# Reordering one step of a convolution stage: TensorE's taps ahead of the rows, the rows' copy behind ScalarE's taps, a silu between two taps

## The chip, the cores and the metric

The kernel runs on one core of one Trainium2 chip. The metric is device microseconds of that core for the whole program. The core's engines work side by side, each through its own list of instructions: TensorE (PE in the profile, with its weight loads as PEld), VectorE (DVE), ScalarE (ACT), GpSimd (POOL) and SyncE (SP), which here only issues DMAs. GpSimd issues DMAs of its own.

## What is computed

Two layers over 8 images of 128 x 128 positions and 128 channels, all in float32. The first is a linear attention with a normalisation. The second is a state space layer; its beginning, which the change is about, is a projection to 256 channels, a depthwise 3 x 3 convolution, a silu, and a small projection to 10 rows:

```
xz = x @ Win
xb, z = jnp.split(xz, 2, axis=-1)
xb = jnp.transpose(xb, (0, 3, 1, 2))
xb = jax.lax.conv_general_dilated(xb, conv_w, (1, 1), ((1, 1), (1, 1)), ..., feature_group_count=Cd)
xb = jax.nn.silu(xb + conv_b[None, :, None, None])
xf = xb.reshape(Bb, Cd, L)
xt = jnp.transpose(xb, (0, 1, 3, 2)).reshape(Bb, Cd, L)
xs = jnp.stack([xf, xf[..., ::-1], xt, xt[..., ::-1]], axis=1)
...
x_dbl = jnp.einsum('bcl,cd->bdl', xs_flat, Wxproj)
dt = x_dbl[:, :r]
Bs = x_dbl[:, r:r + N]
Cs = x_dbl[:, r + N:]
```

Four scans over the positions, a gate, a normalisation and an output projection follow.

## The kernel before

The program has three stages: layer0 (to about 2400 us of the profiled span), layer1_front (to about 4540 us) and layer1_scan (the rest). The change is in layer1_front alone.

The front goes through 8 images in 16 pieces of 1024 positions (8 columns of 128), which makes 128 steps n. The 256 channels are two halves, c = 0 and c = 1, of 128 partitions each. A helper, in_order, ties the instructions of every engine to the order in which the program issues them, so the order in step(n) is the order on each engine's queue, SP's and GpSimd's included. An engine that waits holds all that stands behind it.

What is done for a piece n, with the function names and lines:

- load(n) (L481, SP): its columns of x1 into one of two buffers xi.
- project(n, c) (L488, TensorE): into a PSUM tile pxb of which there is one buffer. place(n, c) (L497, ScalarE) copies it into the bordered tile xb, and a second small copy (L502) writes the edge columns shared by the pieces n and n-1, so VectorE's last two taps of piece n-1 need place(n, c).
- The nine taps of the convolution are divided. taps_pe (L515, TensorE) computes two from xi with premultiplied weights into a PSUM tile acc, of which there are two buffers; so the taps of piece n+1 wait for the silu of the same half of piece n. taps_act (L523, ScalarE) scales three shifted copies of xb into tiles tap, and GpSimd adds them up (L525, two additions). taps_dve (VectorE) adds that sum to acc (L531) and does four multiply-adds (L533).
- silu(n, c) (L538, ScalarE) reads acc and writes ures, in which a whole image is kept.
- rows(n) (L547, TensorE) multiplies ures with the 10-row projection into a PSUM tile pr. keep_rows(n) (L551, ScalarE) copies pr into the one tile xd, and SP issues two stores of it (L554). spread(n, hf) (L559, TensorE) turns a row of xd into tiles pb, and by_b(n) (L568, VectorE) multiplies ures with them in place and stores the result (L569, SP). pr, pb and ptx, a tile of turned parts, take turns in two PSUM buffers.
- sum_d(n) (L582, ScalarE) writes du, which is stored or, in 6 of 8 images, added by GpSimd's DMA (L590).
- turn(k) (L605) copies a turned part of the image out of ures, two per step, and store_turned (L612, SP) stores it; two buffers are in turn. In the same 6 of 8 images ScalarE does half of one of the two ("shared").
- In some steps of an image parts of stored rows are loaded (L623), split by GpSimd (L44, L46) or turned by TensorE (L636) and copied by ScalarE (L638), and stored (L646).

step(n) works on several pieces at once: VectorE on n, by_b on n-1, ScalarE's taps on n+1, the load on n+2. In the kernel before, rows(n) stands at the end of step n and keep_rows(n) near the start of step n+1, ahead of ScalarE's taps.

Of the kernel before, what the change touches and what calls it, by code (L numbers as in the profile page):

```python
# [383 lines left out]
def layer1_front(ctx: ExitStack, tc, x1, win, conv_w, conv_b, wxp, d_par, ubs, xds, xps, gs):  # L384
# [20 lines left out]
    ON_ACT = ((-1, -1), (-1, 0), (-1, 1))  # L405
# [8 lines left out]
    def weight(n, c, dw, dh):  # L414
        i = tap(dh, dw) if own(place_of(n)[0]) == TURN else tap(dw, dh)
        return cw[:, c, i : i + 1]
# [54 lines left out]
    def place_of(n):  # L471
        return SEQ[n // NCH % B], n % NCH
# [3 lines left out]
    def load(n):  # L476
        b, g = place_of(n)
        x = xins[n % 2]
        cols = CW + 1 if g < NCH - 1 else CW
        src = x1[b].rearrange("c (w h) -> c w h", h=H)[:, g * CW : g * CW + cols, :]  # L480
        nc.sync.dma_start(x[:, 0:cols, inner], src)  # L481
        if g == NCH - 1:
            nc.gpsimd.memset(x[:, CW, :], 0.0)

    def project(n, c):
        pxs[n, c] = px = pj.tile([P, CW, H], F32, name="pxb", tag="pj")
        for hf in range(2):
            nc.tensor.matmul(  # L488
                px[:, hf * 4 : hf * 4 + 4, :], wi[:, c, :], xins[n % 2][:, hf * 4 : hf * 4 + 4, inner],
                start=True, stop=True,  # L490
            )

    def place(n, c):

        g = n % NCH
        xb = xbs[n % 2]
        nc.scalar.copy(xb[:, c, 1 : CW + 1, inner], pxs.pop((n, c)))  # L497
        if g == 0:
            nc.gpsimd.memset(xb[:, c, 0, :], 0.0)  # L499
        else:  # L500
            dst, src = edges[n % 2]
            nc.scalar.copy(dst[:, c], src[:, c])  # L502
        if g == NCH - 1:
            nc.gpsimd.memset(xb[:, c, CW + 1, :], 0.0)

    def at(n, c, dw, dh):
        return xbs[n % 2][:, c, 1 + dw : 1 + dw + CW, 1 + dh : 1 + dh + H]

    def taps_pe(n, c):
        accs[n, c] = acc = pa.tile([P, CW, H], F32, name="acc", tag="acc")  # L510
        for hf in range(2):
            s = slice(hf * 4, hf * 4 + 4)
            for j, (dw, dh) in enumerate(ON_PE):
                x = xins[n % 2][:, hf * 4 + dw : hf * 4 + dw + 4, 1 + dh : 1 + dh + H]
                nc.tensor.matmul(acc[:, s, :], wt[:, j, c, :], x, start=(j == 0), stop=(j == len(ON_PE) - 1))  # L515

    def taps_act(n, c):
        for j, d in enumerate(ON_ACT):
            if j:
                t = wp.tile([P, CW, H], F32, name="tap", tag="tb", bufs=4)  # L520
            else:
                t = wp.tile([P, CW, H], F32, name="tap", tag="ta", bufs=2)
            nc.scalar.activation(t, at(n, c, *d), AF.Copy, scale=weight(n, c, *d))  # L523
            if j:
                nc.gpsimd.tensor_tensor(sums[n, c], sums[n, c], t, ALU.add)  # L525
            else:
                sums[n, c] = t

    def taps_dve(n, c):
        acc = accs[n, c]  # L530
        nc.vector.tensor_tensor(acc, sums.pop((n, c)), acc, ALU.add)  # L531
        for d in ON_DVE:
            nc.vector.scalar_tensor_tensor(acc, at(n, c, *d), weight(n, c, *d), acc, ALU.mult, ALU.add)  # L533

    def silu(n, c):
        g = n % NCH
        u = ures[:, c, g * CH : g * CH + CH]
        nc.scalar.activation(u, accs.pop((n, c)).rearrange("p w h -> p (w h)"), AF.Silu, bias=cb[:, c : c + 1])  # L538

    def rows(n):  # L540

        g = n % NCH
        prs[n] = p = pm.tile([2 * 32, 512], F32, name="pr", tag="m")
        for c in range(NC2):
            for hf in range(2):
                u = ures[:, c, g * CH + hf * 512 : g * CH + hf * 512 + 512]
                nc.tensor.matmul(p[32 * hf : 32 * hf + 32, :], wx[:, c, :], u, start=(c == 0), stop=(c == NC2 - 1))  # L547

    def keep_rows(n):
        b, g = place_of(n)  # L550
        nc.scalar.copy(xd[0:64, :], prs.pop(n))  # L551
        for hf in range(2):
            s = slice(g * CH + hf * 512, g * CH + hf * 512 + 512)
            nc.sync.dma_start(xds[b][:, s], xd[32 * hf : 32 * hf + R + 2, :])  # L554

    def spread(n, hf):
        pbs[n, hf] = p = pm.tile([P, 1, 512], F32, name="pb", tag="m")
        sel = ident[:, 32 * hf + R : 32 * hf + R + 1].to_broadcast([P, P])
        nc.tensor.matmul(p[:, 0, :], sel, xd, start=True, stop=True)  # L559

    def by_b(n):

        b, g = place_of(n)
        dst = ubs[b, own(b)].rearrange("c p l -> p c l")
        for hf in range(2):
            s = slice(g * CH + hf * 512, g * CH + hf * 512 + 512)
            u = ures[:, :, s]
            nc.vector.tensor_tensor(u, u, pbs.pop((n, hf)).to_broadcast([P, NC2, 512]), ALU.mult)  # L568
            nc.sync.dma_start(dst[:, :, s], u)  # L569
# [14 lines left out]
    def store_sum(n):  # L584
        if place_of(n)[0] in SEQ_FIRST:
            nc.sync.dma_start(sums_at(n), dus.pop(n))

    def add_sum(n):
        if place_of(n)[0] not in SEQ_FIRST:
            nc.gpsimd.dma_start(sums_at(n), dus.pop(n), accum_op=ALU.add)  # L590
# [6 lines left out]
    def turn(k, copies, tag, bufs):  # L597
        m, r = divmod(k, COPIES)
        hf = m % 2
        c, i = divmod(r, COPIES // NC2)  # L600
        turned[k] = t = wp.tile([P, 2 * 8, HALF], F32, name="turned", tag=tag, bufs=bufs)
        rows = 16 // len(copies)
        for j, copy in enumerate(copies):
            r0 = 16 * i + rows * j
            copy(t[:, rows * j : rows * j + rows], uturn[:, c, r0 : r0 + rows, hf * HALF : hf * HALF + HALF])  # L605

    def store_turned(k):
        m, r = divmod(k, COPIES)
        b, hf = SEQ[m // 2], m % 2
        c, i = divmod(r, COPIES // NC2)  # L610
        dst = ubs[b, 1 - own(b)][c].rearrange("p (g e q) -> p g e q", e=2, q=8 * HALF)[:, 2 * i : 2 * i + 2, hf, :]
        nc.sync.dma_start(dst, turned.pop(k).rearrange("p (g h) w -> p g (h w)", g=2))  # L612

    def shared(n):
        return 0 <= n < N and place_of(n)[0] not in SEQ_FIRST
# [25 lines left out]
    def store_parts():  # L641
        while parts:
            q, r0, rows, order, p = parts.pop(0)
            dst = xps[SEQ[q], order if own(SEQ[q]) == NAT else 1 - order].rearrange("j r (a e) -> a j r e", e=P)
            for j in range(3):
                nc.sync.dma_start(dst[:, j, r0 : r0 + rows, :], p[:, j])  # L646
# [16 lines left out]
    def step(n):  # L663

        live, then, later, before = 0 <= n < N, 0 <= n + 1 < N, 0 <= n + 2 < N, 1 <= n <= N
        b, g = place_of(n)
        ka, kb = 2 * (n - 8) - 1, 2 * (n - 8)
        if live:
            taps_dve(n, 0)
        if ka >= 0:  # L670
            turn(ka, [nc.gpsimd.tensor_copy], "tc", 2)
        if before:
            add_sum(n - 1)
        if before:
            keep_rows(n - 1)
        if live:
            taps_pe(n, 1)
        if later:
            load(n + 2)
        if then:  # L680
            project(n + 1, 1)
            taps_act(n + 1, 0)
            place(n + 1, 1)
        store_parts()
        if before:
            store_sum(n - 1)
        for k in sorted(turned):
            if k != ka:
                store_turned(k)
        if before:  # L690
            for hf in range(2):
                spread(n - 1, hf)
        if live:
            silu(n, 0)
        if then:
            taps_pe(n + 1, 0)
        if later:
            project(n + 2, 0)
        if live:
            taps_dve(n, 1)  # L700
        if then:
            taps_act(n + 1, 1)
        if ka >= 0:
            store_turned(ka)
        if before:
            by_b(n - 1)
        if live:
            silu(n, 1)
        if later:
            place(n + 2, 0)  # L710
        if live:
            rows(n)
            sum_d(n)
        if kb >= 0:
            turn(kb, [nc.gpsimd.tensor_copy, nc.scalar.copy] if shared(n) else [nc.gpsimd.tensor_copy], "tc", 2)
        split_step(n)
# [19 lines left out]
    with in_order(tc):  # L736
        for n in range(-2, N + 1):
            step(n)
        tail()
# [523 lines left out]
```

## Time and profile before

| | |
|---|---|
| median of 3 runs | 9363.71 us (9353.22 to 9363.73) |
| profiled execution | 9364.78 us, span 9363.0 us |
| busy in the span | DVE 85%, POOL 78%, ACT 76%, PE 68% |
| stretch 3400 to 3800 us (in the front) | DVE 354.73, PE 350.49, ACT 345.20, POOL 337.89 us busy of 400; DMA 0.84 |
| front, first and last L531 of VectorE | 2407.45 and 4522.59 us |

Shares over the whole span mix three stages with different limits; for this change only the stretch of the front counts. There all four engines are busy for 84% to 89% of the time, so that none is clearly the limit, and the order of the work and the waits between the engines set the length of a step. A step is about 16.5 us: (4522.59 - 2407.45) / 128. A row of the waits names who waited, for whom, and for how long in total. This one is SyncE's, whose issue of a store stands for a while in every step before ScalarE has copied the rows:

```profile
SPq L554 <- ACT xd L551: 761.2, 128, 18.4
```

The columns are total us, times, longest us.

### The profile page before, as it was taken

Reading aid. Unit: us, or ns where it says so; the run is one execution under the profiler, and the core shown is the slowest. Engines: PE = TensorE matmul, PEld = TensorE weight load, DVE = VectorE, ACT = ScalarE, POOL = GpSimd, SP = SyncE. Lnnn points to the kernel's source line nnn. Section 1 sums busy time; section 2 is a strip of 40 time slices with the busy share of each in tenths; the row PEclk is TensorE's granted clock in tenths of the full one; section 3 lists DMA queues with packets and bytes.
Section 4 is the critical chain, followed back from the end, with each engine's and each line's share of the span. In section 5 each row is a group of like instructions: output and inputs, shape, how many; then the busy total and the mean of one; then the engine's idle time right before and its main releaser. Section 6 shows DMA issues by size and latency. Waiting matters only on the chain. (4 is left out here: it accounts for less than half of the span.)

```text
span 9363.0 us, 91413 instructions
## 1 busy us (share of the span) xinstructions
PE 6381.8 (68%) x24512; PEld 3145.7 (34%) x24512; DVE 7997.6 (85%) x7953; ACT 7096.1 (76%) x8066; POOL 7319.3 (78%) x4684
## 2 busy tenths in 40 slices
PE   8899998998888988888434636436364363643636
PEld 5555555554333333333101403114031140321403
DVE  6667666674799988888799999999999999999996
ACT  5555555658788888888688787887888878788885
POOL 3446444465688888888589899998999989999997
PEclk9999999999999999999655756657575575665857
DMA  1322333223477788888757759578595785967858
GB/s 75 144 91 90 134 118 144 105 80 143 159 240 239 249 233 230 234 233 225 215 155 208 234 169 260 166 204 239 167 267 166 206 234 165 252 175 200 248 165 216
DMA packets 934771, 1750.67 MB, mean 187 GB/s; under 512 B 150229, under 2 KB 376149, under 8 KB 926065
## 3 DMA queue, kind: packets, MB, share of 16 engines
q1 hardware_dynamic: 873328, 1509.92, 48.8%
q0 software_dynamic: 60928, 234.90, 13.5%
q8 instruction: 200, 3.28, 0.1%
q14 instruction: 315, 2.57, 0.1%
HBM read 1052.36 MB, written 692.12 MB: 186 GB/s over the span
## 5 line engine op out<-in xcount | busy, mean ns | idle before, releaser
L946 POOL TENSOR_TENSOR h<-ubt,sp 128x1024 f32<-128x1024 f32 x1024 | 2416.1, 2388 | 371.0 <-DMA rows<-xps 110.2
L929 PE MATMUL px<-rows,dtw 128*128 128x512 bf16 x2048 | 955.2, 565 | 2267.5 <-DVE y L996 1069.8
L525 POOL TENSOR_TENSOR tap<-tap 128x1024 f32<-128x1024 f32 x512 | 1211.2, 2366 | 299.1 <-ACT tap L523 278.8
L533 DVE SCALAR_TENSOR_TENSOR acc<-xb,cw,acc 128x1024 f32<-128x1024 f32 x1024 | 1320.6, 1290 | 76.1 <-ACT xb L502 28.2
L933 ACT ACTIVATE sp<-px 128x1024 f32<-128x1024 f32 x1024 | 1046.4, 1023 | 433.0 <-PE px L929 412.8
L929 PEld LDWEIGHTS <-dtw 128*128 128x128 bf16 x2048 | 168.3, 110 | 3090.0 <-issue 1019.3
L956 DVE TENSOR_TENSOR_SCAN h<-px,h 128x1024 f32<-128x1024 f32 x512 | 1177.8, 2332 | 32.0 <-ACT px L937 15.7
L954 DVE TENSOR_TENSOR_SCAN h<-px,h 128x1024 f32<-128x1024 f32 x512 | 1178.5, 2332 | 21.3 <-POOL h L946 18.4
L1004 POOL TENSOR_TENSOR y<-y,h 128x512 f32<-128x512 f32 x768 | 1158.6, 1550 | 3.9 <-DVE h L977 3.9
L515 PE MATMUL acc<-xi,wt 128*128 128x512 f32 x2048 | 985.4, 625 | 194.8 <-ACT ures L538 194.8
L937 ACT ACTIVATE px<-sp,sa 128x1024 f32<-128x1024 f32 x1024 | 1110.4, 1109 | 6.1
L523 ACT ACTIVATE tap<-xb,cw 128x1024 f32<-128x1024 f32 x768 | 825.2, 1140 | 16.7 <-POOL xb L499 16.5
L282 POOL TENSOR_TENSOR q<-q,qs 128x512 f32<-128x512 f32 x256 | 271.7, 1061 | 694.6 <-DVE qs L281 694.6
L933 ACT ACT_TABLE_LOAD x512 | 656.9, 1283 | 166.1 <-PE px L929 144.6
L937 ACT ACT_TABLE_LOAD x512 | 656.9, 1283 | 9.3
L515 PEld LDWEIGHTS acc<-xi,wt 128*128 128x128 f32 x2048 | 381.2, 196 | 772.0 <-issue 471.2
L1069 PEld LDWEIGHTS px<-wg,z 128*128 128x128 f32 x4096 | 595.9, 232 | 114.1 <-issue 108.0
L1069 PE MATMUL px<-wg,z 128*128 128x128 f32 x4096 | 594.3, 315 | 0.0
L962 PE MATMUL pc<-rows,csel 128*128 128x512 bf16 x1024 | 521.0, 589 | 75.0 <-DVE rstd L1057 71.1
L488 PE MATMUL pxb<-xi,wi 128*128 128x512 f32 x1024 | 487.2, 598 | 39.1 <-DMA xi<-x 36.9
L996 DVE TENSOR_TENSOR y<-y,px 128x1024 f32<-128x1024 f32 x384 | 468.7, 1221 | 14.4
L298 ACT ACTIVATE sq<-o 128x512 f32<-128x512 f32 x256 | 161.2, 630 | 421.4 <-DVE o L296 420.1
(153 smaller groups left out, 15040.3 us busy)
## 6 DMA issues: line engine op xcount, KB each, us to landing
ubt<-ubs SPq DMA_DIRECT2D x1024, 512.0 KB
zs<-z SPq DMA_DIRECT2D x512, 256.0 KB
ubs<-ures SPq DMA_DIRECT2D x256, 512.0 KB
ubs<-turned SPq DMA_DIRECT2D x256, 512.0 KB
z<-zs SPq DMA_DIRECT2D x256, 512.0 KB
y<-gs POOLq DMA_DIRECT2D x128, 1024.0 KB, 10.5
gs<-du POOLq DMA_DIRECT2D x96, 1024.0 KB, 8.8
rows<-xps SPq DMA_DIRECT2D x1536, 60.0 KB
```

The source lines that it names most:

```text
L515: nc.tensor.matmul(acc[:, s, :], wt[:, j, c, :], x, start=(j == 0), stop=(j == len(ON_PE) - 1))
L523: nc.scalar.activation(t, at(n, c, *d), AF.Copy, scale=weight(n, c, *d))
L525: nc.gpsimd.tensor_tensor(sums[n, c], sums[n, c], t, ALU.add)
L533: nc.vector.scalar_tensor_tensor(acc, at(n, c, *d), weight(n, c, *d), acc, ALU.mult, ALU.add)
L929: nc.tensor.matmul(p[:, hf * 512 : hf * 512 + 512], sl.dw[:, c * P : c * P + P], src, start=True, stop=True)
L933: nc.scalar.activation(t, da[n, c], AF.Softplus)
L937: nc.scalar.activation(da[n, c], sp[n, c], AF.Exp, scale=sa[:, sl.s, c : c + 1])
L946: nc.gpsimd.tensor_tensor(h, u, t, ALU.mult)
L954: nc.vector.tensor_tensor_scan(e[:, ::-1], x[:, ::-1], e[:, ::-1], start, ALU.mult, ALU.add)
L956: nc.vector.tensor_tensor_scan(e, x, e, start, ALU.mult, ALU.add)
L1004: nc.gpsimd.tensor_tensor(v[:, c], v[:, c], h[:, c], ALU.add)
L1069: nc.tensor.matmul(po[:, w, :], z[:, c, w * H : w * H + H], wg[:, c, :], start=(c == 0), stop=(c == NC2 - 1))
```

## The change

Four instructions or groups of them move in step(n); none is added or removed.

- rows is no longer issued at the end of its own step but in the next one, as rows(n - 1), behind taps_pe(n, 1) and ahead of load(n + 2) and project(n + 1, 1).
- keep_rows(n - 1), with its ScalarE copy and its two DMA issues on SP, moves from ahead of taps_pe(n, 1) to behind taps_act(n + 1, 0). On SP it thereby comes behind the load.
- taps_act takes a list of taps. The taps of the second half are issued as two and one, and silu(n, 1) stands between.

```
-    def taps_act(n, c):
-        for j, d in enumerate(ON_ACT):
+    def taps_act(n, c, some=range(len(ON_ACT))):
+        for j in some:
+            d = ON_ACT[j]
...
         if before:
             add_sum(n - 1)
-        if before:
-            keep_rows(n - 1)
         if live:
             taps_pe(n, 1)
+        if before:
+            rows(n - 1)
         if later:
             load(n + 2)
         if then:
             project(n + 1, 1)
             taps_act(n + 1, 0)
+        if before:
+            keep_rows(n - 1)
+        if then:
             place(n + 1, 1)
...
         if then:
-            taps_act(n + 1, 1)
+            taps_act(n + 1, 1, (0, 1))
         if ka >= 0:
             store_turned(ka)
         if before:
             by_b(n - 1)
         if live:
             silu(n, 1)
+        if then:
+            taps_act(n + 1, 1, (2,))
         if later:
             place(n + 2, 0)
         if live:
-            rows(n)
             sum_d(n)
```

More of the change, by code (lines that the diff above doesn't have):

```diff
@@ L515, in taps_pe, with taps_act @@
                 nc.tensor.matmul(acc[:, s, :], wt[:, j, c, :], x, start=(j == 0), stop=(j == len(ON_PE) - 1))
-    def taps_act(n, c):
-        for j, d in enumerate(ON_ACT):
+    def taps_act(n, c, some=range(len(ON_ACT))):
+        for j in some:
+            d = ON_ACT[j]
             if j:
@@ L673, in step @@
             add_sum(n - 1)
-        if before:
-            keep_rows(n - 1)
         if live:
             taps_pe(n, 1)
+        if before:
+            rows(n - 1)
         if later:
@@ L682, in step @@
             taps_act(n + 1, 0)
+        if before:
+            keep_rows(n - 1)
+        if then:
             place(n + 1, 1)
@@ L701, in step @@
         if then:
-            taps_act(n + 1, 1)
+            taps_act(n + 1, 1, (0, 1))
         if ka >= 0:
@@ L708, in step @@
             silu(n, 1)
+        if then:
+            taps_act(n + 1, 1, (2,))
         if later:
@@ L711, in step @@
         if live:
-            rows(n)
             sum_d(n)
```

## The prediction

> **What bounds the kernel now.** I read the page first (busy shares in 40 slices), then the groups of the stretch 2400 to 4535 us, which holds all of the front, by engine, then the timeline of two of its steps. The change touches only the front: its 128 steps run from 2407 to about 4533 us of a span of 9363.0 us. In these groups the columns after the bars are busy us, mean ns, idle us before the group and who ended that idling.
>
> ```profile
> L533 DVE SCALAR_TENSOR_TENSOR acc<-xb,cw,acc 128x1024 f32<-128x1024 f32 x1024 | 1320.6, 1290 | 76.1 <-ACT xb L502 28.2 <-DVE acc L533 0.9
> L531 DVE TENSOR_TENSOR acc<-tap,acc 128x1024 f32<-128x1024 f32 x256 | 314.2, 1227 | 145.3 <-PE acc L515 121.7 <-POOL turned L605 11.7 <-POOL tap L525 11.3
> L568 DVE TENSOR_TENSOR ures<-ures,pb 128x1024 f32<-128x1024 f32 x254 | 297.9, 1214 | 0.0
> L497 ACT COPY xb<-pxb 128x1024 f32<-128x1024 f32 x256 | 258.0, 1008 | 255.0 <-PE pxb L488 253.6
> L515 PE MATMUL acc<-xi,wt 128*128 128x512 f32 x2048 | 985.4, 625 | 194.8 <-ACT ures L538 194.8
> L488 PE MATMUL pxb<-xi,wi 128*128 128x512 f32 x1020 | 483.7, 596 | 39.1 <-DMA xi<-x 36.9 <-ACT xb L497 2.1
> ```
>
> VectorE is the busiest engine and waits mostly for TensorE's taps (121.7 us). But ScalarE waits 253.6 us for TensorE's projection, and TensorE 194.8 us for ScalarE's silu: those two wait for each other, which is a loop. The timeline of one fast step shows it (columns: start us, us, engine, line):
>
> ```profile
> 3606.92 5.40 PE L515 MATMUL acc<-xi,wt 128*128 128x512 f32 x8 [2.06 <-ACT ures L538]
> ...
> 3614.07 1.02 ACT L497 COPY xb<-pxb 128x1024 f32<-128x1024 f32 x1 [3.09 <-PE pxb L488]
> 3615.12 0.41 ACT L502 COPY xb<-xb 128x256 f32<-128x256 f32 x1
> 3615.43 2.18 ACT L582 ACTIVATE du<-ures,sd 128x1024 f32<-128x1024 f32 x2
> 3617.52 1.07 ACT L605 COPY turned<-ures 128x512 f32<-128x512 f32 x1
> 3618.50 0.58 ACT L551 COPY xd<-pr 64x512 f32<-64x512 f32 x1
> 3618.97 3.23 ACT L523 ACTIVATE tap<-xb,cw 128x1024 f32<-128x1024 f32 x3
> 3619.86 0.38 SPq L481 DMA_DIRECT2D xi<-x  x1
> 3621.06 1.88 PE L559 MATMUL pb<-xd,ident 128*128 128x512 f32 x4
> 3622.11 1.00 ACT L497 COPY xb<-pxb 128x1024 f32<-128x1024 f32 x1
> 3623.45 1.11 ACT L538 ACTIVATE ures<-acc,cb 128x1024 f32<-128x1024 f32 x1
> 3624.61 3.70 PE L515 MATMUL acc<-xi,wt 128*128 128x512 f32 x8 [1.67 <-ACT ures L538]
> 3628.14 1.88 PE L488 MATMUL pxb<-xi,wi 128*128 128x512 f32 x4
> 3630.06 1.01 ACT L497 COPY xb<-pxb 128x1024 f32<-128x1024 f32 x1 [1.39 <-PE pxb L488]
> ```
>
> Call P the start of place(n+1,0), 3614.07. ScalarE then works without a gap until the first silu ends at 3624.56 (P+10.49); TensorE runs taps of the first half and the projection to 3630.03; the next P is 3630.06. The loop is 15.99 us, 10.5 of ScalarE and 5.5 of TensorE. VectorE repeats in 15.3 us where nothing holds it (2955.60 to 2970.85 in its timeline). Three things lengthen the loop. A copy of turned parts (L638, 0.79) is in it in 5 of 16 steps, net 0.7. The clock is the second: L515's eight matmuls take 5.40 instead of 3.70 us after a gap of 2.05 to 2.08 us (22 cases of 31 with such a gap, none of 95 after 1.68 or less), 22 x 1.70 = 37 us. The third is the load: L488 waits 36.9 us for xi in 39 steps.
>
> Check: in the 96 steps in which ScalarE helps with the turned copies, 96 x 15.99 + 30 x 0.7 + 37 + 37 = 1630 us. VectorE's timeline gives 267.3 us for steps 16 to 31 and 1345.7 for 48 to 126, and one more of about 16.5 makes 1630. The 32 other steps take 15.3 to 15.6 and are VectorE's.
>
> **What the Trainium skill says.** *TensorE: Matmul & The Clock Gate*, Part 1 (the HAM clock gate): the array runs at half rate after an idle window of about 3.4 us and needs about 3.4 us of activity to come back. The cost agrees: one window at half rate loses 1.7 us, the trace's 5.40 - 3.70. The trigger doesn't: here gaps of 2.05 do it and 1.67 don't; I use the trace's. The same page's specifications call ScalarE's queue strictly first in, first out, so a silu that waits holds the tap behind it; the trace shows starts in program order. *DMA: Bandwidth & Descriptors*, Queues, rings and completion order: descriptors of one issuer are consumed in ring order. So a load issued ahead of SP's stores is read ahead of them; the trace shows the issue order (load at 3619.86, turned stores at 3622.57), not the order inside the ring.
>
> **The change part by part**, from P.
>
> *TensorE's order.* Before: project(n+1,0), rows, taps of the second half, project(n+1,1), spread, ends at P -0.03, 1.8, 5.4, 7.2, 8.9. After: the taps come first and end at P+3.6, rows 5.5, project(n+1,1) 7.2. Same work. The taps need the acc buffer of silu(n-1,1), which ended (3609.88 + 1.10) long before P. So VectorE's "PE acc" wait on the second half goes; what is late next there is the edge copy L502 of place(n+1,1), which its third multiply needs and which ends at P+9.5. VectorE then does two multiplies (2.6), by_b (2.3) and is at P+14.4, when the taps of the first half (P+10.54 + 3.70) are done: a tie. So nothing of the 121.7 us comes out directly; the loop sets the step.
>
> *keep_rows behind the three taps.* ScalarE's sum is unchanged, silu still ends at P+10.5. The copy starts at 18.50 + 3.14 = 3621.6 (P+7.6) and rows are done at P+5.5, so no new wait. Behind it stand place(n+1,1), whose projection is done at 7.2 for a start at 8.0, and silu. spread reads xd and now starts at about P+8.2, ends at 10.1; the next taps start at 10.54. Margin 0.44 us, beside ScalarE's place and silu. TensorE's gap of 1.67 (2.05 with the copy of parts) becomes about 1.0 (1.5) before spread and 0.45 behind it. Neither reaches the 2.05 at which the clock fell: all 37 us go. From both sides: 0 to 37 saved, I take 37; a fall at the shorter gaps is the slower rival.
>
> *Queues.* On SP the load now stands before keep_rows' two issues: it waits only for the second half's taps (P+3.6) and goes out at about P+3.9 instead of P+5.8 (3619.86), 1.9 earlier. The longest xi wait was 2.1, the usual 1.3 to 1.4, so nearly all 36.9 us could go. DMA is busy 84% there, so the load may land less than 1.9 earlier: 0 to 36.9, I take three quarters, 28. The two issues of keep_rows go out at P+8.2 instead of 5.0; behind them on SP stand the stores of parts (2.2 us) and both turned stores, 3622.57 becomes about 3625.2, 2.6 later. Who waits for these: the next turned copies on GpSimd (3631.77, 0.25 us late by the store) and ScalarE (3633.51, in the loop, 1.8 of margin). But 1 MB of turned data then meets a queue that had the load 1.9 earlier, so I expect the landing 0 to 1 later: no cost; the other end is a rival. GpSimd's own DMA and its order are unmoved; its tap sums can start 0.47 earlier.
>
> *silu(n,1) before the third tap.* ScalarE is at it at P+12.55 instead of 13.6. VectorE is done with the second half at about P+12.1, so no wait. The third tap ends at 14.7; GpSimd's first sum runs from 12.65 to 15.05 and covers it. place(n+2,0) comes at 15.99. Saves nothing, costs nothing; hidden by the 1.39 wait. Where VectorE is late (1.29 and 0.51 at 2667 and 2682) the tap slips by as much, in steps that VectorE sets.
>
> *PSUM.* rows, spread and the turned parts share two buffers; each new tile follows a by_b or ScalarE read that has ended by then. by_b overwrites what rows reads, at P+12 against 5.5.
>
> Sum: -37 - 28 = -65 us on the profiled execution's 9364.78, 9300. The median of the runs, 9363.71, is 1 us away.
>
> **Rivals.** *Half of it*: the load waits behind a DMA queue that is full at the shorter step, or the clock still falls: -37, 9328. For it: 84% DMA; against: DMA is nearly idle (share 0.04) at 3616 to 3620. *Stores late*: landing 2.6 later takes the 1.8 of margin and 0.8 more, 96 x 0.8 = 77 us in the loop, which eats both savings: 9365. Against: the same bytes drain in the same time. *More*: if the loop fell under VectorE's 15.3, a further 0.7 x 96 = 67: 9233. Against: nothing leaves the loop. *Slower*: the clock falls at the new gap before spread. At half rate spread takes 3.6 instead of 1.9, 1.26 over the margin: 96 x 1.26 = 121, less 37 and 37, +47: 9412. It decides from 59 of 96 steps on. Against: 57 gaps of 1.57 to 1.68 without a fall; for: idle time now comes twice within 3.4 us.
>
> **How the numbers follow.** Forecast 0.50 (9280 to 9320), half 0.20, more 0.04, stores late 0.12, slower 0.14. Faster 0.74, same 0.12, slower 0.14; within 0.2% is about what a measurement of this kernel can tell from no change. The range 9275 to 9372 leaves out "more" and "slower", 0.18.
>
> **What would show it.** Right: L515 never 5.4 us in the steps; L488's xi wait under 10 us; the "PE acc" wait of L531 mostly gone, L533's wait for L502 larger; shared steps of 16.0 and 16.7; spread (L559) waiting for ACT xd about 1 us a step. Wrong: L559 at half clock; ScalarE's L605 waiting for ubs<-turned; a step still of 17.

## The result and the profile after

The changed kernel takes 9276.7 us (median of 5 runs, 9273.03 to 9288.8) where the kernel before took 9360.26 (5 runs beside it): ratio 0.9911, 95% interval 0.9897 to 0.9924, so 83.6 us less. The profiled execution took 9288.8 us, its span is 9287.0 us, 76 less than the 9363.0 of before.

The front alone is measured more closely by VectorE's first tap instruction of step 0 and of step 127 in the timeline (L531 before; one line was added, so it is L532, and L533 is L534, L538 is L539, L559 is L560): 2406.50 to 4432.60 us, 2026.1, against 2108.7 before. That is 82.6 us less. The rest of the profiled span took 6.6 us more. The change doesn't touch that part, and the five runs of the changed kernel lie up to 16 us apart.

The groups of the front by engine, which answer to those shown of before:

```profile
L534 DVE SCALAR_TENSOR_TENSOR acc<-xb,cw,acc 128x1024 f32<-128x1024 f32 x1024 | 1320.3, 1289 | 133.6 <-ACT xb L502 89.8 <-DVE acc L534 0.9
L532 DVE TENSOR_TENSOR acc<-tap,acc 128x1024 f32<-128x1024 f32 x256 | 313.4, 1224 | 13.1 <-POOL tap L526 10.7 <-PE acc L515 2.0
L497 ACT COPY xb<-pxb 128x1024 f32<-128x1024 f32 x255 | 257.8, 1011 | 154.4 <-PE pxb L488 153.0
L515 PE MATMUL acc<-xi,wt 128*128 128x512 f32 x2048 | 937.6, 600 | 53.6 <-ACT ures L539 53.6
L488 PE MATMUL pxb<-xi,wi 128*128 128x512 f32 x1020 | 492.7, 605 | 2.1 <-ACT xb L497 2.1
L560 PE MATMUL pb<-xd,ident 128*128 128x512 f32 x512 | 255.1, 621 | 112.1 <-ACT xd L552 111.1
```

The wait of L488 for the load of xi is gone altogether (36.9 us before, in the row that the prediction shows). L515 is busy for 47.8 us less, with the same 2048 matmuls. In before's clock record 23 stretches of the front's steps ran at half clock, some 1.7 us lost in each, which is 39 us; in the changed kernel there is none behind the first step. The other 9 us are probably no gain: L488 is busy for 9.0 us more in turn, and the profile's ends of matmuls are modelled. VectorE's wait for TensorE's taps fell from 121.7 to 2.0 us, and most of it turned into a wait for the edge copy L502, 28.2 to 89.8. TensorE now waits 111.1 us for the rows' copy ahead of spread. ScalarE still waits 153.0 us for the projection: the loop of the two engines is still there.

TensorE's timeline of one ordinary step shows the two gaps that took the place of one (last column: idle before, and who ended it):

```profile
3608.57 3.60 PE L515 MATMUL acc<-xi,wt 128*128 128x512 f32 x8
3612.09 1.91 PE L548 MATMUL pr<-ures,wx 128*32 128x512 f32 x8
3613.93 1.99 PE L488 MATMUL pxb<-xi,wi 128*128 128x512 f32 x4
3616.96 1.98 PE L560 MATMUL pb<-xd,ident 128*128 128x512 f32 x4 [1.04 <-ACT xd L552]
3619.32 3.70 PE L515 MATMUL acc<-xi,wt 128*128 128x512 f32 x8 [0.38 <-ACT ures L539]
```

Shared steps are those of the 6 images in which ScalarE helps with the turned copies. They now take 15.99 to 16.03 us, and 16.7 us where the copy of parts is in the loop; only the first steps behind an image that isn't shared and the steps at the change of an image are out of line. The 95 intervals of shared steps take 1534.4 us (1613.0 before), the 32 others 491.7 (495.7 before).

Step by step, the 78.6 us of the shared steps fall into three parts: 34.4 are waits for xi, 39.1 are the 23 half-clock stretches at 1.7 us, and 5.1 are left over, of which 3.5 lie in the last step of an image. Of the 23 stretches 22 lay in steps with the copy of parts; those take 16.7 us now where they took 18.4.

### The profile page after: what moved, and what is told of

It is laid out like the page before. It is cut to its first block, busy times and chain, and to the rows that moved or that the text cites. A ratio compares the mean times of both kernels' runs of the same rounds, so it can differ in the third digit from the quotient of the medians.

```text
span 9287.0 us, 91371 instructions
## 1 busy us (share of the span) xinstructions
PE 6364.4 (69%) x24512; PEld 3119.9 (34%) x24512; DVE 7986.4 (86%) x7953; ACT 7097.3 (76%) x8066; POOL 7316.7 (79%) x4684
## 4 chain that ended last, share of the span: by engine, by line
DVE 36%; PE 5%; DMA 3%; issue 3%; POOL 2%; ACT 1%; DVEq 0%; SPq 0%; POOLq 0%; ACTq 0%
DVE h L961 10%; DVE h L959 10%; DVE y L1001 4%; DVE h L982 4%; DVE px L989 3%; PE px L1074 3%; DMA out<-r 3%; DVE r L1080 2%; DVE px L993 1%; POOL h L951 1%; PE pm L1042 1%; PE pq L1054 0%; PE pc L967 0%; POOL y L1009 0%; POOL z L1029 0%
## 5 line engine op out<-in xcount | busy, mean ns | idle before, releaser
L534 DVE SCALAR_TENSOR_TENSOR acc<-xb,cw,acc 128x1024 f32<-128x1024 f32 x1024 | 1320.3, 1289 | 133.6 <-ACT xb L502 89.8
L961 DVE TENSOR_TENSOR_SCAN h<-px,h 128x1024 f32<-128x1024 f32 x512 | 1177.4, 2331 | 31.6 <-ACT px L942 15.4
L515 PE MATMUL acc<-xi,wt 128*128 128x512 f32 x2048 | 937.6, 600 | 53.6 <-ACT ures L539 53.6
L515 PEld LDWEIGHTS acc<-xi,wt 128*128 128x128 f32 x2048 | 374.7, 189 | 573.9 <-issue 411.5
L488 PE MATMUL pxb<-xi,wi 128*128 128x512 f32 x1024 | 495.6, 606 | 2.1 <-ACT xb L497 2.1
```

The source lines that it names most:

```text
L961: nc.vector.tensor_tensor_scan(e, x, e, start, ALU.mult, ALU.add)
```

## The experiments

P is the start of place(n+1,0) on ScalarE, as in the prediction. "Front" is the time from VectorE's first tap instruction of step 0 to that of step 127 in each profiled execution; it leaves out the variation of the rest.

| run | median us | ratio to before, 95% | front us | xi wait us | half-clock stretches |
|---|---|---|---|---|---|
| before | 9357.86 to 9367.29 (medians beside the runs) | 1 | 2108.7 | 36.9 | 23 |
| changed kernel | 9276.7 | 0.9911 (0.9897 to 0.9924) | 2026.1 | 0 | 0 |
| e1 no silu edit | 9277.94 | 0.9908 (0.9894 to 0.9921) | 2025.9 | 0 | 0 |
| e2 silu edit alone | 9366.89 | 1.0005 (0.9997 to 1.0014) | 2114.2 | 52.9 | 15 |
| e3 copy behind the taps alone | 9306.99 | 0.9945 (0.9933 to 0.9958) | 2056.5 | 21.5 | 0 |
| e4 copy ahead, rest changed | 9427.4 | 1.0069 (1.0056 to 1.0082) | 2174.3 | 0 | 15 |
| e5 load behind the rows' stores | 9474.5 | 1.0124 (1.0107 to 1.0141) | 2216.3 | 141.6 | 25 |
| e6 silu first, copy between taps | 9256.24 | 0.989 (0.9875 to 0.9904) | 1995.9 | 0 | 12 |
| e7 silu first, copy behind taps | 9233.21 | 0.9865 (0.9851 to 0.988) | 1974.5 | 0 | 0 |
| e8 as e7, no silu edit | 9214.47 | 0.9835 (0.9818 to 0.9852) | 1969.3 | 0 | 0 |

Half-clock stretches are those, from the start of step 1 to that of step 127, for which the clock record of the trace holds half rate.

**The silu edit, taken back (e1) and alone (e2).**

```
-            taps_act(n + 1, 1, (0, 1))
+            taps_act(n + 1, 1)
...
             silu(n, 1)
-        if then:
-            taps_act(n + 1, 1, (2,))
```

> The changed kernel with the second silu back behind all three of ScalarE's taps. Loop theory (ScalarE's work from the placed copy to the first silu, then TensorE's taps and projection, set the step): the silu stands in ScalarE's 1.39 us wait for the projection, so nothing moves: 9277 within 10, steps of 16.0 and 16.7 us, no clock loss, no wait for xi. Rival (the earlier second silu frees the acc buffer sooner and brings part of the gain): 15 to 40 us slower than the changed kernel, and TensorE's taps of the second half wait for that silu.

> The kernel before with only the second silu put between ScalarE's second and third tap. Loop theory: as before, 9360 within 10; the wait for xi stays at about 37 us and some 20 groups of L515 still take 5.4 us. Rival (the silu brings part of the gain): 9320 to 9345.

Both times are as the loop theory has them. Without the edit the front is 2025.9 us against 2026.1; with it alone the time can't be told from before. In e2 the parts moved against each other, though, which wasn't expected: the xi wait rose to 52.9 us instead of staying at 37, and the clock fell 15 times instead of some 20, about 16 us more and 14 less than before. In the changed kernel the edit does nothing for the time: it moves the silu inside ScalarE's wait for the projection. That wait is 153.0 us against 165.8 in e1, and ScalarE's wait for VectorE ahead of the silu 20.0 against 8.4.

**The rows' copy behind ScalarE's taps alone (e3).** TensorE's order is that of before.

```
-        if before:
-            keep_rows(n - 1)
         if live:
             taps_pe(n, 1)
...
             taps_act(n + 1, 0)
+        if before:
+            keep_rows(n - 1)
+        if then:
             place(n + 1, 1)
```

> The kernel before with only the rows' copy (and its two stores) moved behind ScalarE's three taps; rows stay ahead of TensorE's taps. Loop theory: spread now stands in TensorE's idle time, no gap reaches 2 us, so the clock loss of 37 us goes; the load still waits for the later taps (about P+5.5 against P+5.8), so the waits for xi stay or grow somewhat as the steps get shorter: 9320 to 9345, xi wait 25 to 60 us, no group of L515 at 5.4 us. VectorE theory (the gain is VectorE's 121.7 us of waiting for TensorE's taps, ended by the taps standing ahead of the rows): 9350 to 9360, since the order of taps and rows is that of before.

Faster than expected, 9307, because the xi wait didn't stay: it fell to 21.5 us. The waits of VectorE and TensorE in e3:

```profile
DVE acc L531 <- PE acc L515: 88.0, 92, 3.0
```

```profile
PE pb L559 <- ACT xd L551: 108.6, 100, 1.4
PE acc L515 <- ACT ures L538: 54.1, 122, 4.1
PE pxb L488 <- DMA xi<-x: 21.5, 32, 1.3
```

No window at half clock is left, so this part alone brings the clock's 37 to 39 us and some 15 of the load's. VectorE still waits 88.0 us for TensorE's taps, and the kernel is 54 us faster all the same. The front is 52.2 us shorter than before; TensorE's new order, and the earlier load with it, brings the other 30.4 (2056.5 to 2026.1; the silu edit counts for nothing by e1), of which 21.5 are the rest of the xi wait. In that second part 86 us of VectorE's wait go, from 88.0 to 2.0, and at most 9 us of time can be put down to them. VectorE waits for the edge copy instead (18.6 us in e3, 89.8 in the changed kernel): its wait for the taps wasn't the cause.

**The copy put back ahead of ScalarE's taps in the changed kernel (e4).**

```
+        if before:
+            keep_rows(n - 1)
         if then:
             project(n + 1, 1)
             taps_act(n + 1, 0)
-        if before:
-            keep_rows(n - 1)
-        if then:
             place(n + 1, 1)
```

> The changed kernel with the rows' copy put back ahead of ScalarE's taps (the load stays ahead of its stores). Loop theory: the copy waits for the rows, P+5.5 instead of P+4.4, which is 1.1 us of ScalarE in the loop; spread follows the projection without a gap, so TensorE's idle time is one gap of about 2.5 us and the clock falls in nearly every shared step, 1.7 us each: 9277 + 96 x 2.8 = 9545, steps near 18.8 us; with the clock falling in only half of them 9465. If the clock has no part, only the 1.1 us: 9277 + 96 x 1.1 = 9383. VectorE theory: the taps stand ahead of the rows, so the gain stays: about 9280.

Slower than before by 0.69%, although TensorE's taps stand ahead of the rows and xi never waits: the VectorE theory, which put it at 9280, is out. It is under the 9465 to 9545 of the loop theory with the clock and over its 9383 without. ScalarE has a new wait:

```profile
ACT xd L552 <- PE pr L548: 117.7, 127, 2.2
```

That is 0.93 us a step. An ordinary shared step goes from 16.00 to 16.85 us. The loop now also outlasts VectorE in the other 32 steps, which I hadn't counted: they go from about 15.3 to 16.85 as well. The clock took less than expected. The gap of TensorE is 2.53 us in nearly every step, and yet the clock fell only 15 times. Two such gaps, from TensorE's timeline and in windows of 3.41 us (columns: the window, its length, the busy time of PE, PEld, DVE, ACT and POOL with their instructions; the last three are granted clock, DMA share, GB/s; only PE and the clock matter here):

```profile
3525.20 1.88 PE L560 MATMUL pb<-xd,ident 128*128 128x512 f32 x4
3529.60 5.16 PE L515 MATMUL acc<-xi,wt 128*128 128x512 f32 x8 [2.53 <-ACT ures L539]
...
3611.29 1.88 PE L560 MATMUL pb<-xd,ident 128*128 128x512 f32 x4
...
3615.70 3.70 PE L515 MATMUL acc<-xi,wt 128*128 128x512 f32 x8 [2.53 <-ACT ures L539]
```

```profile
3525.77:3529.19 3.42, 1.30 (x4) 0.23 (x2) 1.82 (x2) 3.39 (x5) 2.86 (x2) 1.00 1.05 199
3529.19:3532.60 3.41, 3.00 (x4) 1.45 (x5) 3.37 (x4) 3.41 (x5) 2.74 (x2) 0.50 1.02 312
3611.11:3614.52 3.41, 2.06 (x5) 0.57 (x3) 1.92 (x2) 3.38 (x5) 3.41 (x3) 1.00 0.64 109
3614.52:3617.94 3.42, 2.24 (x5) 1.05 (x6) 3.23 (x3) 3.42 (x5) 2.95 (x3) 1.00 1.11 213
```

The first gap has 2.11 us in one window of a fixed grid, and the next window ran at half clock (0.50). The second, just as long, is cut by the grid at 3614.52 into 1.35 and 1.18 us, and nothing happens. The same view of the kernel before, for the gap of 2.06 us that the prediction shows:

```profile
3603.79:3607.20 3.41, 1.35 (x4) 0.47 (x3) 2.88 (x3) 3.38 (x5) 3.33 (x2) 1.00 1.06 207
3607.20:3610.62 3.42, 3.42 (x5) 1.36 (x5) 3.41 (x3) 3.42 (x4) 2.77 (x2) 0.50 1.12 283
```

The grid is read from each trace's clock record, whose entries lie multiples of 3.413 us apart. Laid over all steps of before, e2 and e4, the windows behind which the clock fell held 1.91 to 2.37 us of idle PE, the others at most 2.02, by the profile's modelled ends. The other runs fit: in e5 and e6 the clock, when it was at full rate, fell behind windows with 1.98 us or more and behind none with less, and in the changed kernel, e1, e3, e7 and e8, where it never fell, no window held more than 1.83. Every half-clock stretch of before, e2 and e4 is one window of 3.41 us; a step with one is 1.7 us longer in before and 1.4 to 1.7 us longer in e4.

**The load behind the rows' stores (e5).**

```
-        if later:
-            load(n + 2)
...
         if before:
             keep_rows(n - 1)
+        if later:
+            load(n + 2)
```

> The changed kernel with the load put back behind the rows' two stores on SP, so that it goes out at about P+8.9 instead of P+3.9. Loop theory: the load is in TensorE's part of the loop; it lands some 9 us after its issue and is wanted at P+14.2, so TensorE waits 2.5 to 3.7 us in each shared step, and where such a gap falls into one clock window 1.7 more: 9277 + 96 x 2.5 = 9517 up to 9277 + 96 x 5.4 = 9795. Rival (the early load is only a by-product, the DMA queues have room and it lands in 4 to 5 us): within 40 us of the changed kernel.

The direction is the theory's, the size is under its lower end: 198 us more than the changed kernel. The xi wait comes in 61 steps only:

```profile
PE pxb L488 <- DMA xi<-x: 141.6, 61, 4.0
```

Of these, 30 are waits of 3.5 to 4.1 us, five in each shared image, and make 112 us of the total. They follow GpSimd's own DMA, the accumulating one of 1 MB of du (L591). The lines of one long wait and of the next step, where no wait came:

```profile
3301.79 1.20 POOL L591 DMA_DIRECT2D gs<-du  x1
3303.62 0.38 SPq L481 DMA_DIRECT2D xi<-x  x1
...
3312.91 2.58 PE L488 MATMUL pxb<-xi,wi 128*128 128x512 f32 x4 [3.96 <-DMA xi<-x]
...
3319.38 1.20 POOL L591 DMA_DIRECT2D gs<-du  x1 [1.38 <-ACT du L583]
...
3325.12 0.38 SPq L481 DMA_DIRECT2D xi<-x  x1
```

The first load is issued 1.83 us behind that DMA, and the projection starts 9.3 us after the load's issue. The second is issued 5.74 us behind it, and the projection starts without a wait at 3330.27, 5.1 us later. In all shared images it is the same: the projection waits for the 30 loads that go out 1.75 to 3.7 us behind GpSimd's DMA until 8.1 to 9.4 us after their issue, and the 30 loads between them, 5.4 to 6.1 us behind it, are there within 5.3 us. Idle DMA engines just before the issue don't explain the fast ones: the DMA share was 0.00 from 3298 to 3302, ahead of the slow load. That GpSimd's DMA is what slows it is likely, but no run moves that DMA alone.

In the middle of an image long and short steps alternate, 20 to 23 us and 16.0, so my 96 waiting steps were too many. The rival was right on one point: in many steps the load lands in about 5 us. The clock has a part too: of the 25 half-clock stretches 12 are two windows long. No run separates what they cost.

**Further down the loop (e6, e7, e8).** The loop holds place(n+1,1) and its edge copy, 1.35 us, only because they stand ahead of the first silu on ScalarE. e7 changes that order in the changed kernel:

```
         if before:
             keep_rows(n - 1)
+        if live:
+            silu(n, 0)
         if then:
             place(n + 1, 1)
...
-        if live:
-            silu(n, 0)
         if then:
             taps_pe(n + 1, 0)
```

e6 also puts keep_rows(n - 1) between the second and third tap of the first half; e8 is e7 with e1's edit.

> The changed kernel with the first silu ahead of place(n+1,1) on ScalarE, and the rows' copy between its second and third tap so that spread is over when that silu ends. Loop theory: the placed copy and the edges (1.35 us) leave the loop, which falls to 14.65 us plus the 0.7 of the copied parts, under VectorE's 15.3: shared steps of 15.3 to 15.6, 96 x 0.6 to 0.9 less: 9190 to 9220. Rival (the DMA queues, 14.2 us busy in a step, or VectorE's wait for the edge columns, now 1.1 later, become the limit): 9250 to 9285.

> As e6, but the rows' copy stays behind all three taps. Loop theory: spread then ends at about P+10.1, 0.9 after the silu, and TensorE's taps wait for it: loop 15.6 us, 96 x 0.4 = 38 less than the changed kernel: 9240. Rival (spread isn't in the loop): as e6.

> As e7, with the second silu back behind all three of ScalarE's taps. In e7 that silu waited for VectorE in 121 steps, 83.7 us in all, and held the third tap. Loop theory: VectorE sets the ordinary steps (15.38 us) and the wait stands in ScalarE's slack, so nothing is gained or lost: 9233 within 12. Rival (the held tap is in the loop of the steps with the copied parts, 16.05 us there): 9205 to 9225.

All three beat the changed kernel. In e7, 9233 where 9240 was expected, the ordinary shared steps take 15.4 us and those with the copy of parts 16.05 to 16.1, near VectorE's 15.3.

e6 was expected to be the faster one, 9190 to 9220, and missed: 9256 lies in its rival's range, and its front is 21.4 us longer than e7's. ScalarE waits there for the one du buffer, until GpSimd's DMA of du has landed. The row of e6 first, then that of e7:

```profile
ACT du L583 <- DMA gs<-du: 22.0, 17, 2.4
```

```profile
ACT du L583 <- DMA gs<-du: 2.1, 5, 0.6
```

Step against step, the 17 steps of e6 with that wait are 19.7 us longer than in e7. All 12 of e6's falls of the clock lie in such steps, since the wait widens TensorE's gap; they lengthen the steps behind them by 8.6 us in all. The other 98 steps are 6.9 us shorter, 15.26 us where e7 has 15.37, which is what the edit was for. e6 issues its stores about 1 us earlier, beside GpSimd's accumulating DMA of du; that they slow it may be the reason for the wait, but no run separates it.

e8 is the fastest, 0.9835 of before, and misses its expectation of 9233 within 12: its median is 19 us below e7's, in the rival's range. The rival's reason isn't seen: the ordinary steps with the copy of parts take 16.05 us in both. The front shows 5 of the 19 us, a little in many steps, and the rest lies in a part of the program that the edit doesn't touch. Whether the silu edit costs anything in e7 is therefore not settled.

## Why the prediction was right

The loop, right. The prediction said that the step is set by ScalarE's work from P to the first silu and TensorE's taps and projection behind it, 15.99 us, and 0.7 with the copy of parts. The changed kernel's shared steps are 16.0 and 16.7 us. e4, which puts a wait of 0.93 us into that loop, lengthens an ordinary step by 0.85. e7, which takes 1.35 us out of it, shortens one by 0.63, to 15.37, where VectorE's 15.3 is nearly reached.

TensorE's order, right: the "PE acc" wait went (2.0 us left), L502 took its place, and e3 shows that those 121.7 us were not worth their time: at most 9 us for the last 86 of them.

keep_rows, right in its price: no wait on ScalarE for the rows, and TensorE waits for the copy about as foreseen (1.04 and 1.34 us measured, 1.0 and 1.5 expected; 0.38 behind spread, expected 0.45).

The clock, right in the sum and wrong in the rule. All of it went, 37 us as counted and 39 by the clock record, which has one fall more. But "the 2.05 at which the clock fell" isn't a length of gap: e4 has gaps of 2.53 us at full clock. What counts is how much of one 3.41 us window of a fixed grid is idle: from about 2 us on it falls. Splitting a gap of 2.05 into 1.34 and 0.38 with matmuls between leaves at most 1.43 us idle in any window, so the conclusion held. It rested on the wrong rule, and that is luck in part: a single gap shorter than 2 us was safe under both rules, but gaps that add up in one window are not. The rival "slower" saw that danger, two gaps within 3.4 us; here they came to too little. The Trainium skill's free-running window (TensorE: Matmul & The Clock Gate, Part 1) fits the grid, and its 3.4 us the length of it; but a wholly idle window isn't needed, 59% of one was enough here (2.03 of 3.41 in the windows of before).

The load, under-sized. The step that was off is "I take three quarters, 28": all 36.9 us went. The load was issued at P+3.4 to P+3.8, where 3.9 had been foreseen, and before at P+5.5 to P+6.5. That is about 2.4 us earlier instead of 1.9, and more than the longest wait, 2.1. The prediction left out one thing more. "GpSimd's own DMA and its order are unmoved" holds for GpSimd, but the load moved past it. In the step that the prediction shows, GpSimd's DMA of du was issued at 3619.49 and the load behind it at 3619.86; now the load is ahead:

```profile
3612.19 0.36 SPq L481 DMA_DIRECT2D xi<-x  x1
3615.88 1.20 POOL L591 DMA_DIRECT2D gs<-du  x1
```

In the shared steps of the six runs without a wait for xi every load goes out ahead of that DMA of its step. In the four others (before, e2, e3, e5) most or all go out behind it, and only those are waited for. How much of the gain is the earlier issue and how much the place ahead of GpSimd's DMA is open; e5 shows that a late place on SP costs time, and that the load is slow close behind that DMA. That the load lands faster in the changed kernel isn't shown: there it has about 10 us before it is wanted.

So the 82.6 us in the front are the 65 forecast, 9 more for the load, 2 more for the clock and 6.6 that weren't in the sum. Of the last, 3.5 lie in the last steps of shared images and 1.6 in the images that aren't shared; the cause there wasn't tried by itself. The measured 9276.7 is therefore below the 9280 to 9320 given for the forecast itself, and close to the lower end, 9275, of the whole range. The mechanism was right, the gain was put too low.

The stores, right: GpSimd's wait for turned stores to land was 17.8 us in 51 cases before and is 13.8 in 14 now, ScalarE has none in the steps. The silu, right: nothing (e1, e2).

The rivals "half", "stores late" and "slower" are out by the measured time; "more" needed something to leave the loop, and nothing did until e7. In "stores late" the sum is off by a little: 77 less 74 makes 9368 and not 9365.

## What to carry to other kernels

When two engines wait for each other, write down the loop with its instructions and durations before looking at the busiest engine: what is in the loop pays until another engine sets the step, and a wait outside of it, be it 121.7 us, pays next to nothing when it is removed. Reordering can be worth as much through what it does to the issue time of a load (36.9 us) and to the shape of TensorE's idle time (37 us) as through the work that it moves. When a load comes late, look at which DMA of another engine goes out just ahead of it, not only at the share of the DMA engines. If the aim is to shorten a step further, move out of the loop what only stands there by order, as e7 did.

## What was unexpected of the hardware

In all ten traces TensorE's clock changes on a grid of 3.41 us that keeps its phase throughout an execution. A gap of 2.06 us halved the clock for the next window when it lay within one, and one of 2.53 us did not when a grid line cut it. Steps of nearly five windows keep the phase from step to step: in e4 two steps took 16.85 and 17.24 us, 34.1 together, ten windows. So the loss can repeat or stay away for many steps at a time. It isn't always paid, either: in e6 nearly every step with a fall is only as much longer as its wait for du, and a loss of about 0.7 us shows in the next step. In e5 a load of 576 KB was there within 5.3 us in the steps where it went out 5.4 to 6.1 us behind GpSimd's 1 MB accumulating DMA, and only after 8.1 to 9.4 us where it went out 1.75 to 3.7 us behind it, in the same loop.
